# Filling the result with beta's rows: seven transfers moved from GpSimd's queue to SyncE's

## The chip, the cores and the metric

The kernel runs on one core of a Trainium2 chip. The metric is the device time of one execution in microseconds (us). Three executions of the kernel before took 592.14, 590.57 and 588.76 us: the median is 590.57.

## The reference

Two layers of cross attention follow each other. Each takes x (8 batches, 100 rows, 1024 wide) and the same context (8 batches, 1444 rows, 512 wide).

```python
# layer 0
Q = x @ Wq + bq;  K = ctx @ Wk + bk;  V = ctx @ Wv + bv
weights = softmax(Q @ K.T / 32, axis=-1)          # over the context's rows
x = x + (weights @ V) @ Wo + bo
# layer 1
q = x @ Wq + bq;  k = ctx @ Wk + bk;  v = ctx @ Wv + bv
w = softmax(q @ k.T / 32, axis=1)                 # over the 100 query rows
x = w @ v + x
out = (x - mean(x)) * rsqrt(var(x) + 1e-6) * gamma + beta
```

The last line is the one that matters here: beta is added to each row of the result.

## The kernel before, in words

All data is float32. The weights are multiplied together first (Wq with Wk, Wv with Wo), so that the context itself can serve as keys and values. TensorE then goes through layer 0 batch by batch, makes the output product of layer 0 (names o_x, o_y and so on) and the queries of layer 1 (g_x, g_y and so on), goes through layer 1 batch by batch, and ends with output products and the normalisation.

**A batch.** In one pass TensorE makes the scores of a batch against the keys (tile s, line 960, from cT, the context with its features down the partitions) and the rows weighted by the softmax (tile A, line 913, from c, the context with its rows down the partitions). `alternated` (line 1317) lets the two take turns: matmuls of A for batch b stand between matmuls of s for batch b + 2. The first two batches' scores of each layer therefore stand by themselves, ahead of it.

**Loads.** A context block is 1444 by 512, close to 3 MB, and is read anew in each layer in both layouts. `load_features` makes the transfers of cT, `load_rows` those of c; both go through `loaded_in_order` (line 860), which issues them on SyncE's queue and keeps them in program order, so every c and cT load stands at line 861 in the profile. In layer 1 a cT tile comes in four transfers. The tiles live in a pool of ten (`stream`) and one of three (`feature_block`), and SyncE waits before a transfer until TensorE has read what lay there. The built program gives each of SyncE's transfers one of eight DMA semaphores in turn, and each transfer waits for the one that had the semaphore before it, so at most eight of them are on the way.

**The fill.** The result of each batch but the last is stored by GpSimd with an accumulating transfer (line 1247), which adds the normalised rows to what lies in the result. What lies there is beta, written once for seven batches by the transfers of lines 1377 to 1379: each has 100 rows of 1024 (400 KB), all read from the one row of beta in memory, from memory to memory. The last batch is stored by SyncE and ScalarE in two halves (line 1303) and gets its beta from VectorE.

**Order around the change.** On GpSimd's queue stand, in this order: the sums of the softmax weights of layer 0's last batch (lines 1172 to 1177), the seven fills, a memset for the first w of layer 1 (line 972), the load of layer 1's Wv (tile wv, line 1381), two memsets, and from line 185 on the sums of Wv's blocks. On SyncE's queue stand: cT of layer 1's batch 0, cT of batch 1, and then, from `alternated`, by turns c of batch 0 and cT of batch 2, and so on. Two of batch 1's cT tiles are waiting for a buffer that layer 0's output product uses, until 359 us. GpSimd's and SyncE's transfers run on the same 16 DMA engines.

Of the kernel before, what the change touches and what calls it, by code (L numbers as in the profile page):

```python
# [33 lines left out]
B, T, E = 8, 100, 1024  # L34
# [21 lines left out]
def two_layer_cross_attention(ctx: ExitStack, tc: tile.TileContext, a: dict, out: bass.AP):  # L56
    nc = tc.nc
# [10 lines left out]
    def bank(name):  # L68
        return psum.tile([P, 512], F32, tag="ps", name=name)
# [4 lines left out]
    def unit(name):  # L74
        return stream.tile([P, E + L], F32, tag="unit", name=name)
# [7 lines left out]
    def weight_rows(name):  # L83
        return work.tile([P, MC * T], F32, tag="wT", name=name, bufs=3)

    def feature_block(name):
        return work.tile([P, S], F32, tag="prob", name=name, bufs=3)
# [55 lines left out]
    def run(*parts):  # L143

        parts = list(parts)
        while parts:
            parts = [g for g in parts if next(g, parts) is not parts]
# [679 lines left out]
    for g in range(B // G):  # L827
# [3 lines left out]
                out=xT[:, :, g * GT : (g + 1) * GT],  # L831
                in_=a["xT"].rearrange("(c p) t -> p c t", p=P)[:, :, g * GT : (g + 1) * GT],
# [27 lines left out]
    def loaded_in_order(to, src):  # L860
        tc.keep_in_program_order(nc.sync.dma_start(out=to, in_=src))  # L861

    def load_features(b, blocks=(2, 3), parts=2):

        bounds = [LAST * i // parts for i in range(parts)] + [S]

        for k in range(LC):
            name = f"cT_{b}_{k}"
            t = feature_block(name) if k in blocks else unit(name)[:, :S]
            for part in (slice(i, j) for i, j in zip(bounds, bounds[1:])):  # L870
                loaded_in_order(t[:, part], a["ctxT"][b][k * P : (k + 1) * P, part])
            yield t
# [16 lines left out]
    def keys(m):  # L889

        return P if m < MC - 1 else S - LAST
# [3 lines left out]
    def both_sides():  # L895

        return side, 1 - side

    def one_side():

        nonlocal side
        side = 1 - side
        return (1 - side,)
# [40 lines left out]
    def scores_by_keys(s, layer, cT, softmax):  # L944

        b = s["b"]
        q = gT[layer][b // G]
        t0 = b % G * T
        banks = [bank(f"s{layer}_{b}_{n}") for n in range(MC // GM)]
        rest = []  # L950
        for k in range(LC):
            for m in KEYS:
                whole = keys(m) == P
                n = HP if whole else keys(m)
                for h in both_sides() if whole else one_side():
                    o = m * P + h * HP if whole else m * P
                    to = banks[m // GM][h * HP : h * HP + n, m % GM * T : (m % GM + 1) * T]
                    if k >= LC - 2 and not whole:
                        rest.append(to)
                    nc.tensor.matmul(  # L960
                        to,
                        cT[k][:, o : o + n],
                        q[:, k, t0 : t0 + T],
                        start=(k == 0 and m % GM == 0),
                        stop=(k == LC - 1 or (k == LC - 2 and not whole)),
                        skip_group_check=True,
                    )
                if (k, m) != (LC - 1, KEYS[-1]):
                    yield
        w = weight_rows(f"w{layer}_{b}")  # L970
        s["w"] = w[:, : MC * T].rearrange("p (c t) -> p c t", t=T)
        nc.gpsimd.memset(s["w"][:PAD, MC - 1, :], 0.0)  # L972
        s["softmax"] = softmax(s, [blocks_of(banks, ms) for ms in ROWS], rest)
        for _ in islice(s["softmax"], LATER.get((layer, b))):
            pass
        yield

    def blocks_of(banks, ms):

        m, n, r = ms[0], len(ms), keys(ms[0])  # L980
        ps = banks[m // GM][:r, m % GM * T : (m % GM + n) * T]
        return ms, r, ps.rearrange("p (c t) -> p c t", t=T)
# [391 lines left out]
            next(more, None)  # L1374
    run(more)
    vector.in_order = False
    for b in range(B - 1):
        rows = a["L1_xattn_beta"].partition_broadcast(T)
        tc.keep_in_program_order(nc.gpsimd.dma_start(out=out[b], in_=rows))
    wv1 = weights.tile([P, LC, E], F32, tag="w", name="wv1")  # L1380
    nc.gpsimd.dma_start(out=wv1, in_=a["L1_xattn_Wv"].rearrange("(c p) e -> p c e", p=P))


    cT = [list(load_features(0, parts=4)), list(load_features(1, (2,), 4))]
    scores1 = scores_by_keys(batches[0], 1, cT[0], softmax1)
    run(islice(scores1, LC * MC - 2))
    key_bias_rows(kb1, bqbk1)
# [59 lines left out]
```

## Time and profile before

| what | value |
|---|---|
| median of three executions | 590.57 us |
| the profiled execution | 589.33 us |
| its span, first to last instruction | 587.6 us |
| TensorE busy (matmul) | 575.2 us, 98% |
| VectorE, ScalarE, GpSimd busy | 399.6, 133.3, 135.0 us |
| moved by DMA | 142.96 MB, 243 GB/s in the mean |
| the seven fills | issued from 317.5 to 321.4 us, 400 KB each, 9.4 us from issue to landing in the median |
| load of wv | issued at 357.2 us, 10.1 us to landing |
| the last c and cT loads before SyncE's long wait | under way from 359 to about 380 us |

How to read it: the page gives each engine's busy time, then the span cut in 40 slices (14.7 us each) with a digit for the busy tenths. A row of the chain of waits is a start, a length and who held up the end of the program at that moment; "issue" there is time in which an engine waited for nothing that the profile shows. A row of DMA queues is the number of packets, the megabytes, and the time that these packets took as a share of 16 engines over the window. q1 is SyncE's queue, q0 GpSimd's, q10 ScalarE's; q8 and q14 bring instructions. A row of busy time by window gives, for PE, PEld (weight loads), DVE (VectorE), ACT (ScalarE) and POOL (GpSimd), the busy us and the number of instructions, and then TensorE's clock, the DMA engines' busy share and GB/s.

### The profile page before, as it was taken

The numbers are of one execution on the slowest core, as the hardware profiler recorded it, in microseconds if no ns is written. First come the engines' busy times: TensorE is split into PE (matmuls) and PEld (weight loads), VectorE is DVE, ScalarE is ACT, GpSimd is POOL, SyncE is SP. The second block draws the span as 40 slices with busy tenths as digits, with TensorE's granted clock in tenths as the row PEclk, the third lists the DMA queues.
The fourth block names the chain that finished last, engine by engine and source line by source line (L and its number), as shares of the span: only waits on it lengthen the run. The fifth ranks groups of instructions, "written<-read, shape, count | busy, mean of one in ns | idle before, by whom it ended". The sixth has DMA issues, their size and how long they took to land.

```text
span 587.6 us, 17570 instructions
## 1 busy us (share of the span) xinstructions
PE 575.2 (98%) x7470; PEld 497.6 (85%) x7470; DVE 399.6 (68%) x936; ACT 133.3 (23%) x349; POOL 135.0 (23%) x206
## 2 busy tenths in 40 slices
PE   9999999999999999999999899999999999999994
PEld 8887457678899999999998656787999999999992
DVE  1997579879686873876559587876444447664695
ACT  1331321433330112211111000103333303154313
POOL 3110110221111132241225000003922312341052
PEclk9999999999999999999999999999999999999998
DMA  8959989944599999999999605807889997599114
GB/s 274 308 107 321 311 202 296 287 73 97 94 248 360 332 378 365 369 371 366 370 316 289 134 0 206 301 2 222 281 289 304 338 314 258 158 310 328 40 30 85
DMA packets 74313, 142.96 MB, mean 243 GB/s; under 512 B 8572, under 2 KB 30332, under 8 KB 74236
## 3 DMA queue, kind: packets, MB, share of 16 engines
q1 hardware_dynamic: 65790, 117.81, 58.2%
q0 software_dynamic: 8048, 23.57, 19.7%
q8 instruction: 59, 0.97, 0.7%
q10 hardware_dynamic: 398, 0.47, 0.2%
q14 instruction: 18, 0.15, 0.1%
HBM read 124.40 MB, written 6.14 MB: 222 GB/s over the span
## 4 chain that ended last, share of the span: by engine, by line
PE 86%; DMA 6%; SPq 2%; issue 2%; POOL 2%; ACT 1%; DVE 0%; POOLq 0%; DVEq 0%
PE s L960 18%; PE A L913 17%; PE qk_x L166 7%; PE g_x L166 6%; PE o_x L166 5%; PE vo_x L166 4%; DMA cT<-in_ctxT 3%; PE o_y L166 3%; PE g_y L166 3%; DMA c<-in_ctx 3%; PE qk_z L166 2%; PE qk_y L166 2%; SPq L861 2%; PE o_w L166 1%; PE o_z L166 1%
## 5 line engine op out<-in xcount | busy, mean ns | idle before, releaser
L913 PE MATMUL A<-w,c 128*64 128x100 f32 (+1 forms) x3072 | 228.7, 249 | 1.7 <-issue 1.7
L913 PEld LDWEIGHTS A<-w,c 128*64 128x64 f32 (+1 forms) x3072 | 199.1, 137 | 3.6 <-issue 3.3
L960 PE MATMUL s<-g0T,cT 128*64 128x100 f32 (+1 forms) x1472 | 112.7, 249 | 2.0 <-issue 1.9
L960 PE MATMUL s<-g1T,cT 128*64 128x100 f32 (+1 forms) x1472 | 114.1, 249 | 0.1
L960 PEld LDWEIGHTS s<-g1T,cT 128*64 128x64 f32 (+1 forms) x1472 | 97.7, 136 | 2.6 <-issue 1.8
L960 PEld LDWEIGHTS s<-g0T,cT 128*64 128x64 f32 (+1 forms) x1472 | 96.8, 136 | 3.4 <-issue 2.7
L1172 POOL TENSOR_TENSOR part<-w 128x500 f32<-128x500 f32 x16 | 26.4, 1653 | 124.3 <-ACT w L1020 60.9
L1152 ACT ACTIVATE w<-w,negmax 128x100 f32<-128x100 f32 x96 | 35.0, 366 | 68.2 <-DVE negmax L99 68.2
L99 DVE SCALAR_TENSOR_TENSOR w<-s,kb 128x400 f32<-128x400 f32 (+2 forms) x32 | 13.9, 463 | 37.5 <-PE s L960 37.3
L1020 ACT ACTIVATE w<-w 128x400 f32<-128x400 f32 (+2 forms) x32 | 12.0, 442 | 120.3 <-DVE w L99 107.2
L99 DVE TENSOR_REDUCE most<-s 128x100 f32<-128x400 f32 (+1 forms) x24 | 12.5, 520 | 36.5 <-PE s L960 36.5
L166 PE MATMUL qk_x<-qk 128*128 128x256 f32 x128 | 31.0, 392 | 0.0
L166 PEld LDWEIGHTS qk_x<-qk 128*128 128x128 f32 x128 | 24.3, 198 | 3.3 <-ACT qk L440 0.2
L972 POOL MEMSET w<- 68x100 f32 x16 | 3.8, 237 | 75.3 <-PE A L913 36.4
L1232 DVE SCALAR_TENSOR_TENSOR z<-vectors,r,z 100x512 f32<-100x512 f32 x16 | 11.4, 743 | 11.8 <-PE z L1230 11.7
L99 DVE TENSOR_TENSOR w<-w,rtotal 128x400 f32<-128x400 f32 (+2 forms) x32 | 18.3, 570 | 1.1
L1245 ACT ACTIVATE z<-z,rstd 100x1024 f32<-100x1024 f32 x7 | 8.1, 1150 | 45.0 <-POOL rstd L1243 45.0
L1152 ACT ACTIVATION_READ_ACCUMULATOR w<-w,negmax 128x1 f32 x96 | 18.1, 188 | 0.0
L99 DVE TENSOR_TENSOR xT<-xT,o_x 128x400 f32<-128x400 f32 (+1 forms) x32 | 15.9, 538 | 2.8 <-PE o_x L166 2.4
L674 ACT ACTIVATE g1T<-g_x,k 128x400 f32<-128x400 f32 x4 | 2.4, 594 | 61.4 <-PE g_x L166 61.2
L578 POOL DMA_DIRECT2D qk_L_xattn_bk<-qk_L_xattn_bk x6 | 5.2, 922 | 47.8 <-DMA qk_L_xattn_bk<-qk_L_xattn_bk 18.9
L166 PE MATMUL vo_x<-vo 128*128 128x512 f32 x32 | 15.3, 595 | 0.0
(435 smaller groups left out, 1052.7 us busy)
## 6 DMA issues: line engine op xcount, KB each, us to landing
c<-in_ctx SPq DMA_DIRECT2D x176, 256.0 KB
cT<-in_ctxT SPq DMA_DIRECT2D x96, 176.0 KB
cT<-in_ctxT SPq DMA_DIRECT2D x32, 370.0 KB
cT<-in_ctxT SPq DMA_DIRECT2D x32, 352.0 KB
cT<-in_ctxT SPq DMA_DIRECT2D x32, 194.0 KB
vo<-in_L_xattn_Wo SPq DMA_DIRECT2D x8, 512.0 KB
qk<-in_L_xattn_WqT SPq DMA_DIRECT2D x8, 512.0 KB
qk<-in_L_xattn_WqT SPq DMA_DIRECT2D x15, 256.0 KB
```

The lines of the kernel that those rows point to most:

```text
L99: ins = getattr(nc.vector, op)(*args, **kw)
L166: nc.tensor.matmul(banks[n // per][:, n % per * width : (n % per + 1) * width], lhs[i][:, n * P : (n + 1) * P], rhs[i], start=(fresh and i ...
L578: nc.gpsimd.dma_start(out=to, in_=t, accum_op=ALU.add)
L861: tc.keep_in_program_order(nc.sync.dma_start(out=to, in_=src))
L913: nc.tensor.matmul(ps[h * HP : (h + 1) * HP, k * T : (k + 1) * T], c[m // CQ][:r, m % CQ, k * P + h * HP : k * P + (h + 1) * HP], w[:r, m, :],
L960: nc.tensor.matmul(to, cT[k][:, o : o + n], q[:, k, t0 : t0 + T], start=(k == 0 and m % GM == 0), stop=(k == LC - 1 or (k == LC - 2 and no ...
L972: nc.gpsimd.memset(s["w"][:PAD, MC - 1, :], 0.0)
L1020: nc.scalar.activation(rows, rows, AF.Exp)
L1152: nc.scalar.activation(rows[:, i, :], rows[:, i, :], AF.Exp, bias=negmax[:, i : i + 1], accum_out=total[:, i : i + 1])
L1172: add(part, w[:, 0:5, :], w[:, 5:10, :], ALU.add)
L1232: nc.vector.scalar_tensor_tensor(z[:, half], bv1[j][:T], s["r"], ps[:T, :], ALU.mult, ALU.add)
L1245: nc.scalar.activation(z, z, AF.Copy, scale=rstd)
```

## The change

The seven fills leave GpSimd's queue. They are issued by SyncE, in the same way as the context's loads, behind the cT transfers of layer 1's first two batches and ahead of the first c transfer of layer 1. Source, destination, size and number of the transfers stay as they are. The built program has them at that place on SyncE's queue, each with one of the eight semaphores in turn, so that the transfers behind them get other semaphores than before.

```diff
-    for b in range(B - 1):
-        rows = a["L1_xattn_beta"].partition_broadcast(T)
-        tc.keep_in_program_order(nc.gpsimd.dma_start(out=out[b], in_=rows))
     wv1 = weights.tile([P, LC, E], F32, tag="w", name="wv1")
     nc.gpsimd.dma_start(out=wv1, in_=a["L1_xattn_Wv"].rearrange("(c p) e -> p c e", p=P))


     cT = [list(load_features(0, parts=4)), list(load_features(1, (2,), 4))]
+    for b in range(B - 1):
+        loaded_in_order(out[b], a["L1_xattn_beta"].partition_broadcast(T))
     scores1 = scores_by_keys(batches[0], 1, cT[0], softmax1)
```

## The prediction

> **What bounds the kernel now.** The page first: its engine line and the DMA rows by slice.
>
> ```profile
> span 587.6 us, 17570 instructions
> PE 575.2 (98%) x7470; PEld 497.6 (85%) x7470; DVE 399.6 (68%) x936; ACT 133.3 (23%) x349; POOL 135.0 (23%) x206
> ...
> PE   9999999999999999999999899999999999999994
> ...
> DMA  8959989944599999999999605807889997599114
> ```
>
> TensorE is busy 575.2 of 587.6 us, so the whole span holds 12.4 us in which it stands still. One slice before the last shows an 8 (slice 22 counted from 0, 14.7 us each: 323 to 338 us), and in the same slice the DMA row falls from 9 to 6. So I asked the chain of waits, in order of time, for that stretch, and then the timeline of GpSimd.
>
> ```profile
> 319.39 7.70 PE A L913 x175
> 327.09 1.65 issue
> 328.74 1.03 PE A L913 x17
> ```
>
> ```profile
> 317.46 3.85 POOL L1379 DMA_DIRECT2D out<-in_L_xattn_beta  x7
> 329.89 0.18 POOL L972 MEMSET w<- 68x100 f32 x1 [8.58 <-issue]
> ```
>
> The first shows the only stop of TensorE between 221 us and the end that is worth naming: 1.65 us in the last weighted rows of layer 0, "issue", that is with nothing in the profile that it waited for (the list of waits gives TensorE 1.65 us here and 1.9 us in three stops of layer 0, and nothing else past the start). The second shows the seven fills, 3.85 us of issuing on GpSimd. They run while the stop happens. I then asked for the DMA queues in three windows: all of the fills (317 to 335), from 311 to 326, and from 326 to the stop.
>
> ```profile
> q0 software_dynamic: 896, 2.87, 69.8%
> q1 hardware_dynamic: 568, 0.72, 11.1%
> q8 instruction: 2, 0.03, 0.8%
> ```
>
> ```profile
> q1 hardware_dynamic: 2006, 2.57, 52.5%
> q0 software_dynamic: 459, 1.52, 43.2%
> ```
>
> ```profile
> q0 software_dynamic: 72, 0.23, 98.1%
> q8 instruction: 1, 0.02, 7.0%
> ```
>
> q8 brings instructions, 16 KB at a time (0.97 MB in 59 packets on the page; TensorE's 14,940 records over 59 are 253 a block). From 311 to 326 no block comes at all, though TensorE has been eating them since 319.4. One comes at 326 to 327, between fill packets that take 98% of the engines, and TensorE stands from 327.09 until it can be used. Arithmetic: 175 matmuls and as many weight loads in 7.70 us are 45 a us, a block of 256 lasts 5.6 us, two last 11.3 us. From 311 to 327.09 TensorE had used about 64 records of the output products and 350 of these, so it had lived from what was fetched before 311, and then had nothing.
>
> **What the Trainium skill says.** Runtime: NRT & Kernel Launch, section Instruction fetch mechanics: instructions come in 16 KiB blocks of 256 over a DMA queue, fetched ahead while the current ones run; the trace agrees (0.02 MB packets, a stop after two blocks' worth). DMA: Bandwidth & Descriptors, section Queues, rings and completion order: each DMA engine goes round the queues that have work, a whole packet at a time; the trace agrees in so far as the block came late only among fill packets. Same page, Issuing engines are not separate DMA queues: who issues only saves issue time, the engines are the same; so the fills' bytes don't vanish, they move. Same page, Why a DMA increments its semaphore by 16 and not by 1: a transfer from SyncE of 100 rows uses 10 engines, one from GpSimd may use nearly all. The end of the trace agrees: the two 100-row stores there, from SyncE and ScalarE, leave 20 small completion packets, ten each.
>
> ```profile
> DMA packets 221, 0.42 MB, mean 91 GB/s; under 512 B 20, under 2 KB 20, under 8 KB 220
> ```
>
> **The change part by part.**
>
> Removed: seven DMA issues on GpSimd, 3.85 us. Behind them there stand the memset for w and wv1's load. The memset runs at 329.89, just after TensorE's last product of the old w (chain: 328.74 + 1.03); wv1 runs at 357.2 after 27.2 us of waiting for TensorE's o_x. Neither was held by the fills: worth nothing, covered by those waits.
>
> Removed: 2.87 MB of fill packets from 317.5 to about 333. In this stretch SyncE's loads end at 321 and the next wait for buffers until 359, so the DMA engines then stand empty. The instruction block due near 322 (128 records of slow products and A, then 128 more at 45 a us, after the block that the window 309 to 310.5 shows) comes at once. The stop goes: -1.65 us. What is late next there? Nothing that the chain shows; the products behind it (329.9 to 390.8) run back to back. Bounds: 0 if the stop has another cause, -1.65 if all of it goes.
>
> Added: seven issues in SyncE's queue behind cT of the second batch, that is at 366.5 in place of the first c loads of layer 1, some 0.43 us each, 3 us. Queued behind them on SyncE: c and cT of the next batches. Each issue on SyncE also waits for the transfer eight before it (the built program has eight DMA semaphores in turn), so those loads queue behind the fills. Two views tell what that may cost: busy time by window, and SyncE's waits from 359 to 397 us and from 396 to 426.5 us.
>
> ```profile
> 359.00:380.00 21.00, 21.00 (x78) 13.81 (x77) 15.56 (x30) 2.37 (x4) 0.17 (x1) 1.00 0.99 353
> 380.00:397.00 17.00, 17.00 (x192) 14.09 (x193) 13.28 (x23) 2.90 (x6) 0.18 (x1) 1.00 0.01 2
> ```
>
> ```profile
> SPq L861 <- PE s L960: 20.5, 1, 20.5
> ```
>
> ```profile
> SPq L861 <- PE s L960: 28.6, 5, 20.5
> ```
>
> The loads behind the second batch's blocks are done at 379.5; then the DMA is empty for 17 us (share 0.01), because SyncE waits until 396.96 for TensorE to free a block. It waits 28.6 - 20.5 = 8.1 us more, in four pieces, before 426. So the cover is 17.5 + 8.1 = 25.6 us. The first of the loads held up, c of batch 0, is read at 413.9.
>
> How long do the fills take there? Engine time from the row above: 69.8% of 16 engines over 18 us are 201 engine-us, 0.287 us a row of 4 KB. On ten engines that is 20.1 us. The lower bound is ten engines at the rate of the loads of 360 to 380 (362 GB/s by 16): 226 GB/s, 12.7 us. I take 20; both ends lie under 25.6. The loads that ended at 379.5 end at 392 to 400, SyncE's next wait shrinks, and from 426 on nothing differs: cost 0. That cover is not to be wasted: from 426.35 to 475.5 the chain runs over the DMAs and SyncE's queue to a matmul at 475.55, so there a late transfer is paid in full.
>
> Moved: the fills now lie beside instruction blocks of 359 to 390. TensorE takes (78 + 77) records in 21 us there, 7 a us: a block lasts 35 us, and a block late by 5 us costs nothing. From 390.7 on scores run at 45 a us; if fills or held-up loads still fill the DMA then, up to 0.7 us can be lost (the stops of layer 0's scores beside loads were 0.7 at most). From 430 to 470 TensorE lived well with full DMA; I take 0. The later accumulating stores onto the filled rows start at 507, over 100 us after the fills.
>
> Sum: -1.65 us against the profiled execution's 589.33 (span 587.6 and 1.7 around it): 587.7. The three runs have a median of 590.57, 1.24 above it. I set the four executions together, mean 590.2, less 1.65: **588.5 us**.
>
> **The rivals.**
>
> A, as above: 588.5. Chance 0.52; own range 586.8 to 590.2 (half of the 3.4 us over which the runs lie).
>
> B, the stop isn't the fills' doing, or it comes back beside the scores at 390: 590.2. For it: three stops of 0.5 to 0.7 us in layer 0's scores happen with no fills at all. Against: from 430 to 470 eight blocks come (q8 row of that window) with DMA full of loads, and TensorE never stops. Chance 0.14.
>
> C, the stop is longer without the profiler: the runs differ by 3.4 us, the profiled one is near their fast end, and if the difference is this stop, then the median run has 1.65 + 1.24 = 2.9 us of it and all fall to 587.7 or below, with the slowest losing 4.5: 585.7 to 587.7, taken at 587. Chance 0.21. For it: a stop that hangs on where a block lands among 700 rows of fills varies. Against: runs vary by such amounts for other reasons.
>
> D, slower: the fills on ten engines hold back the loads of layer 1. Ten engines read the same beta row, and may need half as long again as on GpSimd's queue, 30.2 us; less the cover of 25.6 that is 4.6 us late at 426, carried by the DMA chain to 475.5: 590.2 - 1.65 + 4.6 = 593.1. It decides from 25.6 us of fills on, and from 27.3 us it beats the gain. Against it: 20.1 us is already the pessimistic reading of the page. Chance 0.13.
>
> That the change doesn't do what it says can be left out: the built program shows the seven transfers on SyncE after cT of batch 1 and gone from GpSimd.
>
> **How the numbers follow.** The bound of 0.5% is 2.95 us, about what a measurement of this kernel can tell from no change: below 587.6 is faster, above 593.5 slower. Faster: of C some 0.16, of A's lower end 0.12: 0.28. Slower: most of D, 0.09. The same: 0.63. Range: 585.8 to 592.2 leaves out D's upper part and the ends of C, some 0.15.
>
> **What would show it.** Right: no "issue" stop near 327; an instruction block near 322; fills of 13 to 20 us that start near 365; the DMA row full until 392 to 400 and SyncE's wait of 20.5 us cut by as much; the first A of layer 1 at 412, 1.65 us earlier. Wrong: the stop stays at 327 without fills (B); TensorE waits for c or cT between 414 and 480, or SyncE no longer waits for TensorE before 426 (D).

## The result, and the profile after

The changed kernel takes 587.86 us (median of 15 runs, 585.15 to 589.50), the kernel before 590.57 us (median of 15 runs beside it, 588.19 to 596.78). The ratio is 0.9953, with a 95% interval of 0.9935 to 0.9971: 2.8 us less, give or take 1.1. Each experiment below has its own runs of the kernel before beside it (medians 590.28, 591.12 and 591.59 us), and a ratio is taken only from runs within 1.5% of the fastest of their kernel, so it is not the quotient of two printed medians. The prediction was 588.5 us in a range of 585.8 to 592.2, with no change beyond 0.5% as the likeliest class.

The page of the changed kernel, the same rows as before:

```profile
span 584.2 us, 17566 instructions
PE 573.8 (98%) x7470; PEld 497.0 (85%) x7470; DVE 399.8 (68%) x936; ACT 133.3 (23%) x349; POOL 131.4 (22%) x199
...
PE   9999999999999999999999999999999999999994
...
DMA  8959989944499999999998006767889997699114
```

The 8 in TensorE's row is gone, and the DMA row, which showed 6 0 in slices 22 and 23, now shows 0 0: the fills have left that stretch. GpSimd has seven instructions less. The chain of waits of the changed kernel from 308 to 334 us:

```profile
310.40 2.88 PE o_x L166 x8
...
318.74 8.39 PE A L913 x192
...
327.31 2.88 PE o_x L166 x8
```

The last A of layer 0 now runs through, 192 matmuls in 8.39 us. Before, the same 192 took 7.70 + 1.65 + 1.03 = 10.38 us. So the stop cost 1.99 us, a little more than the 1.65 us shown as "issue", because the 17 matmuls behind it were slow too. The DMA queues of the changed kernel from 311 to 326 us:

```profile
q1 hardware_dynamic: 2070, 2.66, 52.4%
q8 instruction: 1, 0.02, 0.5%
```

Before, this window held no instruction block (q8); now there is one, and a narrower window puts its start between 320 and 321 us.

The pair of profiles differs by 3.4 us. The starts in the chain tell where. The first o_x starts at 310.40 in place of 311.05: 0.65 us that lie ahead of anything the change touches. The o_x behind A starts at 327.31 in place of 329.95: another 1.99 us, the stop. The last rows of the middle stretch (wsum_ps) come at 476.43 in place of 479.73: 0.66 us more, from the stretch in which before's chain ran over the DMAs. In the other two profiles of the kernel before (below) that last piece is missing, so I count it as chance.

In the new place, SyncE's own waits from 350 to 397 us in the changed kernel (name of the waiting engine and line, of the one waited for, then us in total, times, longest):

```profile
SPq L861 <- PE o_q_x L166: 39.5, 1, 39.5
SPq L861 <- DMA out<-in_L_xattn_beta: 8.0, 5, 2.4
SPq L861 <- PE s L960: 7.2, 1, 7.2
```

The wait for TensorE's scores, 20.5 us before, has become 7.2. SyncE waits 8.0 us for the fills instead, as its eight semaphores come round. TensorE waits for nothing from 310 to 480 us.

### The profile page after: what moved, and what is told of

Read it like the earlier page. It is cut to its first block, busy times and chain, and to the rows that moved or that the text cites. A ratio compares the mean times of both kernels' runs of the same rounds, so it can differ in the third digit from the quotient of the medians.

```text
span 584.2 us, 17566 instructions
## 1 busy us (share of the span) xinstructions
PE 573.8 (98%) x7470; PEld 497.0 (85%) x7470; DVE 399.8 (68%) x936; ACT 133.3 (23%) x349; POOL 131.4 (22%) x199
## 4 chain that ended last, share of the span: by engine, by line
PE 95%; POOL 2%; issue 1%; ACT 1%; DVE 0%; POOLq 0%; DVEq 0%
PE s L960 22%; PE A L913 21%; PE qk_x L166 7%; PE g_x L166 6%; PE o_x L166 5%; PE vo_x L166 4%; PE o_y L166 3%; PE g_y L166 3%; PE qk_z L166 2%; PE qk_y L166 2%; PE o_w L166 1%; PE o_z L166 1%; PE qk_w L166 1%; PE vo_z L166 1%; PE vo_y L166 1%
## 5 line engine op out<-in xcount | busy, mean ns | idle before, releaser
L913 PE MATMUL A<-w,c 128*64 128x100 f32 (+1 forms) x3072 | 228.0, 249 | 0.0
L913 PEld LDWEIGHTS A<-w,c 128*64 128x64 f32 (+1 forms) x3072 | 201.8, 137 | 2.0 <-issue 1.6
L960 PEld LDWEIGHTS s<-g0T,cT 128*64 128x64 f32 (+1 forms) x1472 | 99.9, 136 | 3.0 <-issue 2.4
```

What stands on the lines that cost most here:

```text
L913: nc.tensor.matmul(ps[h * HP : (h + 1) * HP, k * T : (k + 1) * T], c[m // CQ][:r, m % CQ, k * P + h * HP : k * P + (h + 1) * HP], w[:r, m, :],
L960: nc.tensor.matmul(to, cT[k][:, o : o + n], q[:, k, t0 : t0 + T], start=(k == 0 and m % GM == 0), stop=(k == LC - 1 or (k == LC - 2 and no ...
```

## Experiments

Theory F is the prediction's: the fills' packets delay an instruction block that TensorE needs, and the new place is covered. The rivals: the stop has another cause (N), GpSimd's queue costs at any time (Q), the stop varies (C), and the new place costs (D).

**Without the fills.** The kernel before with lines 1377 to 1379 left out, so beta's rows are missing in the result.

```diff
-    for b in range(B - 1):
-        rows = a["L1_xattn_beta"].partition_broadcast(T)
-        tc.keep_in_program_order(nc.gpsimd.dma_start(out=out[b], in_=rows))
```

> Leaves the seven fills out altogether (beta's rows are then missing under the accumulating stores). Theory F (the fills' packets on GpSimd's queue delay the instruction block that TensorE needs near 322 us, and the new place costs nothing): no stop near 327, and the time of the changed kernel, 0.995 of before, within 0.001. If the new place costs something too: faster than the changed kernel, 0.991 or below. Theory N (the gain has nothing to do with a stop at 327): any time, with the stop at 327 still there.

Measured: 586.95 us, ratio to before 0.9954 (0.9936 to 0.9972), the same as the changed kernel. No stop: its chain has "319.42 8.39 PE A L913 x192". So what the fills cost in their old place is all that can be had, and the new place costs nothing that these runs can tell. (Both ratios carry about 1.1 us either way, so a cost of up to some 1.5 us would not show.) D falls for seven fills.

**The fills on GpSimd, but later.** Behind wv1's load, so that they are issued from 356.6 to 360 us.

```diff
+    wv1 = weights.tile([P, LC, E], F32, tag="w", name="wv1")
+    tc.keep_in_program_order(
+        nc.gpsimd.dma_start(out=wv1, in_=a["L1_xattn_Wv"].rearrange("(c p) e -> p c e", p=P))
+    )
     for b in range(B - 1):
         rows = a["L1_xattn_beta"].partition_broadcast(T)
         tc.keep_in_program_order(nc.gpsimd.dma_start(out=out[b], in_=rows))
-    wv1 = weights.tile([P, LC, E], F32, tag="w", name="wv1")
-    nc.gpsimd.dma_start(out=wv1, in_=a["L1_xattn_Wv"].rearrange("(c p) e -> p c e", p=P))
```

> The fills stay on GpSimd's queue, but behind wv1's load, so that they start at 358 us. Theory F: it is the time and not the queue; TensorE takes 7 instructions a us there, no stop of 1 us or more, 0.995 of before. Theory Q (GpSimd's queue itself is what costs, at any time): the gain is lost, 0.999 to 1.001, with a stop between 358 and 400 us.

Measured: 587.55 us, 0.9966 (0.9947 to 0.9985), A in 8.39 us, no stop between 310 and 400. The same queue with the same bytes, 40 us later, does no harm that shows: TensorE takes (70 + 69) instructions in the 18 us from 357 on, some 8 a us, against 45 in A. Q falls.

**ScalarE at the old time.**

```diff
+    for b in range(B - 1):
+        rows = a["L1_xattn_beta"].partition_broadcast(T)
+        tc.keep_in_program_order(nc.scalar.dma_start(out=out[b], in_=rows))
     next(o0)
     next(queries1)
     run(o0)
```

with the three lines on GpSimd taken out.

> The fills at the old time, but issued by ScalarE (from 312 us on, behind its last exponential of layer 0). Theory F in its wide form (fill packets of any queue delay the block): a stop near 327 of 0.5 to 2 us stays, 0.998 to 1.000 of before. In its narrow form (only the packets of GpSimd's queue do): no stop, 0.995.

Measured: 588.38 us, 0.9969 (0.9947 to 0.9990), A in 8.39 us. No stop, as the narrow form has it. But ScalarE issued its fills one by one from 312.9 to 329.5 us, some 2.8 us apart, too thin a stream to settle it.

**SyncE at the old time.** Seven at once, ahead of the cT tiles that wait for a buffer, with the three lines on GpSimd taken out.

```diff
-    cT = [list(load_features(0, parts=4)), list(load_features(1, (2,), 4))]
+    cT = [list(load_features(0, parts=4))]
+    second = load_features(1, (2,), 4)
+    cT.append([next(second), next(second)])
+    for b in range(B - 1):
+        loaded_in_order(out[b], a["L1_xattn_beta"].partition_broadcast(T))
+    cT[1] += second
```

> SyncE issues the seven fills at the old time, ahead of the two cT tiles that wait for a buffer until 359 us, so that up to seven are on the way at once from about 316 us on. Theory F in its wide form (fill packets of any dense queue delay the instruction block; ScalarE's had been too thin): the stop near 327 comes back, 1.5 us or more, 0.998 to 1.000 of before. In its narrow form (only packets on GpSimd's queue delay it): no stop, 0.995 to 0.997.

Measured: 587.42 us, 0.9941 (0.9921 to 0.9962). The DMA queues from 321 to 333 us, this kernel first and then the kernel before:

```profile
q1 hardware_dynamic: 691, 2.56, 58.9%
q8 instruction: 2, 0.03, 1.1%
```

```profile
q0 software_dynamic: 744, 2.35, 89.9%
q8 instruction: 1, 0.02, 0.6%
```

As many fill bytes in the same twelve microseconds, and two instruction blocks come instead of one. Its chain has the whole A in one piece again:

```profile
319.50 8.39 PE A L913 x192
```

So of the two forms the narrow one has the stop right. But "no stop" is not "no delay": SyncE's fills held the block up too, by less than TensorE could bear (the table behind the next experiment). Why GpSimd's hold it up longer is open: on SyncE's queue the fills hold ten engines of 16 (58.9% is close to 10/16), on GpSimd's nearly all (89.9%), and these runs don't separate the queue from the engines it fills.

**Three at the old time, four at the new.**

```diff
-    for b in range(B - 1):
+    for b in range(3):
         rows = a["L1_xattn_beta"].partition_broadcast(T)
         tc.keep_in_program_order(nc.gpsimd.dma_start(out=out[b], in_=rows))
...
+    for b in range(3, B - 1):
+        loaded_in_order(out[b], a["L1_xattn_beta"].partition_broadcast(T))
```

> Three fills stay on GpSimd at the old time, four are issued by SyncE at the new place. Theory F: three fills are through by about 325 us; the block comes some 2 us late in place of 4, which its slack of about 3 us covers: no stop, 0.995 to 0.996. If the cost goes with the number of fills: a stop of 0.7 us, 0.998.

Measured: 588.52 us, 0.9978 (0.9954 to 1.0002): unclear by the time. The profile is clearer: "319.34 8.39 PE A L913 x192", no stop at all. A backlog of three is covered by what TensorE has fetched ahead, seven are not. The cost is not in proportion to the fills.

**Where the block lands in all these kernels.** The traces have every block's packet on q8. Counted from the first matmul of the last A of layer 0, the next block starts and lands at these times:

| fills on the way beside this A | block starts, us | block has landed, us |
|---|---|---|
| none (seven profiles) | 1.9 to 2.1 | 2.9 to 3.3 |
| from ScalarE, one by one | 3.0 | 4.0 |
| from SyncE, seven at once | 3.6 | 4.8 |
| from GpSimd, three | 5.1 | 6.1 |
| from GpSimd, seven (three profiles) | 6.9 to 7.8 | 8.1 to 9.3 |
| from GpSimd, fourteen | 7.7 | 8.9 |

TensorE is through with its 175 matmuls after 7.7 us. In the last two rows the block lands later than that, TensorE stops, and it goes on 1.0 to 1.3 us after the landing; in all other rows the block lands sooner, and there is no stop. So fills from every queue delay the block, GpSimd's the most (about 5 to 6 us for seven, against 1.5 to 2 for SyncE's), and the wide form of F has the delay right. An estimate from the chain says when the block is asked for: 350 records of this A run before the stop, and less a block of 256 that leaves 94, at 45 a us the first 2.1 us. That is where the block starts when no fills are beside it, so it is as if the fetch began when TensorE enters the block before it.

**The kernel before, profiled twice more, and the changed one once more.** No edit.

> The kernel before, unchanged, profiled once more. If the stop hangs on where the block lands among the fills by chance (rival C): a stop near 327 anywhere from 0 to 4 us. If its length is set by the order of the queues: 1.4 to 2.0 us again, at the same matmul.

> The kernel before, unchanged, profiled a third time. Theory F: the stop after the 175th matmul of the last A, 1.6 to 2.2 us; the second loss, that of the first o_x behind it, in some profiles and not in others (0 or about 1.7 us).

> The changed kernel, unchanged, profiled once more. Theory F: no stop between 310 and 400 us. The stops of layer 0 between 190 and 245 us are free to differ by 1 to 2 us from the first profile; if they do, they and not the change are what spreads the runs.

One execution each: 588.28, 591.34 and 585.89 us. The chain of waits from 308 to 334 us of the second profile of before:

```profile
317.00 7.70 PE A L913 x175
324.69 2.13 issue
326.82 1.03 PE A L913 x17
...
328.03 4.58 PE o_x L166 x8
```

and of the third, from 315 to 345 us:

```profile
318.55 7.70 PE A L913 x175
326.25 2.49 issue
328.74 1.03 PE A L913 x17
...
329.96 4.51 PE o_x L166 x8
```

The stop comes after the 175th matmul in every profile that has seven fills on GpSimd at the old time, at whatever time it comes, so it hangs on an instruction and not on a moment. Counted over TensorE's matmuls and weight loads it is behind the 7762nd record each time. The "issue" stops of layer 0 of 0.3 us and more in these three profiles come behind records 2174, 2683, 2938, 3192 and 4716. From one of these to the next, and from the last to 7762, it is 2, 1, 1, 6 and 12 times 254 records, to within two; the prediction had counted 253 records a block. So all these stops lie at the edge of an instruction block, those of layer 0, which rival B named, as well.

The length of the stop varies, 1.65, 2.13, 2.49 us. And in two of three profiles there is a second loss that is not shown as waiting at all: the eight products o_x behind A take 4.58 and 4.51 us where they take 2.88 in every other profile, 1.6 to 1.7 us more. The windows show what it is. First the second profile of before, then the first one:

```profile
328.20:331.60 3.40, 3.40 (x6) 1.74 (x6) 3.25 (x6) 0.00 (x0) 0.00 (x0) 0.50 0.62 135
```

```profile
330.00:333.00 3.00, 3.00 (x9) 1.70 (x10) 2.93 (x6) 0.00 (x0) 0.07 (x1) 1.00 0.64 150
```

TensorE's granted clock (the third number from the end) is 0.50 for 3.4 us, in the third profile too, from 329.8 on; at half the clock, 3.4 us cost 1.7. In the other twelve profiles the clock is 1.00 here. Both stretches begin 1.1 to 1.4 us after TensorE goes on, so they look like a consequence of the stop. But after a stop of 2.21 us (next experiment) none follows, and these runs don't show what decides. All in all the three profiles lose 1.99, 4.2 and 4.5 us (all rows of A and o_x against 8.39 and 2.88), a mean of 3.5. The changed kernel's second profile shows A in 8.39 and o_x in 2.88 us.

**The fills twice at the old place.** `for b in [*range(B - 1), *range(B - 1)]:` at line 1377; the second set writes the same rows again.

> GpSimd issues the seven fills twice over at the old place (the second set writes the same rows again), so that fill packets last from 317 to about 347 us. Theory F: the stop near 327 as before, 1.6 to 2.2 us, and now each later block that TensorE needs before 347 us comes late too: one or two more losses of about 1.7 us, like the one at 331 us in the second profile of the kernel before: 1.000 to 1.005 of before. If the cost went with the bytes: 1.004 to 1.005. If it is one fixed stop: 1.000.

Measured: 591.01 us, 1.000 (0.9983 to 1.0017), with this chain:

```profile
319.66 7.70 PE A L913 x175
327.36 2.21 issue
329.57 1.03 PE A L913 x17
...
330.78 2.88 PE o_x L166 x8
```

The same stop, no more. The block behind it comes late too, at 339.8 us, 10 us after TensorE went on, but these products take few instructions, and TensorE never waits for it. The other 2.87 MB, issued up to 335 us, cost nothing: the loss doesn't go with the bytes.

**The fills twice and three times at the new place.** The loop over `range(B - 1)` in the changed kernel runs over it two or three times.

> SyncE issues the seven fills twice over at the new place (the second set writes the same rows again), so that 14.7 us of fills on ten engines become about 29. By the prediction's cover of 25.6 us: SyncE no longer waits for TensorE before 426, loads come 3 to 4 us late, TensorE waits for them between 440 and 480: 1.005 of the changed kernel, 1.000 to 1.002 of before. If the cover is larger: 0.995 to 0.997 of before. If the fills cost in proportion at this place: slower than before by more than 0.3%.

> SyncE issues the seven fills three times over at the new place, some 44 us of fills. By the kernel with two sets, whose fills lasted 30 us and used up all of SyncE's waits for TensorE before 426 without a stop of TensorE: 14 us more must show as TensorE waiting for c or cT between 400 and 480 us, 10 to 16 us in all, 1.015 to 1.025 of before. If fills at this place are hidden without limit: 0.996 to 1.000.

Twice: 589.16 us, 0.9987 (0.9962 to 1.0012), between what was expected of the two covers; its runs spread from 586.4 to 594.6, and its profile (586.76 us) has no wait of TensorE for a load. SyncE waits for TensorE's scores for 0.2 us in all from 396 to 426.5: the cover is used up almost to the last. Three times (four runs): 602.41 us, 1.0201 (1.0169 to 1.0233), and TensorE waits:

```profile
PE s L960 <- DMA cT<-in_ctxT: 9.5, 5, 3.2
```

The DMA queues of this kernel from 376 to 396 us, where nearly nothing but fills is on the way:

```profile
DMA packets 1112, 4.15 MB, mean 207 GB/s; under 512 B 102, under 2 KB 102, under 8 KB 1111
...
q1 hardware_dynamic: 1111, 4.13, 63.8%
```

4.13 MB are 1008 rows; 63.8% of 16 engines for 20 us are 204 engine-us, 0.202 us a row. Ten engines of 16 are 62.5%: the ten are busy without a break. By that rate seven fills take 700 times 0.202 by 10, 14.2 us. From the first 4 KB packet to the last, the traces have 14.9 us for one set, 30.3 for two and 43.8 for three. The ratios 1.0201 and 0.9953 put three sets 14.6 us behind one set. Taken as it is, that leaves a cover of about 29 us. But only 9.5 of the 14.6 us are waits for cT. Another 3.4 are lost in two stretches of 3.4 us at a granted clock of 0.50 (from 416.8 and from 474.8 us), which follow the two longest waits, and the rest I can't place. By the waits alone the cover is about 34 us. Two sets lie near its lower end: the profiled execution has no wait, and three of the four slowest have mean clocks of 0.990 and 0.993, so these probably did stop.

**ScalarE in the empty stretch.** With the three lines on GpSimd taken out:

```diff
+    after_A = const.tile([P, 1], F32, tag="after_A", name="after_A")
+    tc.keep_in_program_order(nc.scalar.copy(after_A, A0[1][:, 0, GT - 1 : GT]))
+    for b in range(B - 1):
+        rows = a["L1_xattn_beta"].partition_broadcast(T)
+        tc.keep_in_program_order(nc.scalar.dma_start(out=out[b], in_=rows))
     next(o0)
```

> ScalarE issues the fills at 331 us: a one-column copy ahead of them waits for the last A of layer 0. They then lie in the stretch from 331 to 357 us in which the DMA engines are empty, and SyncE's loads don't queue behind them. Theory F: no stop, 0.994 to 0.995 of before, the same as the changed kernel, since its loads were covered anyway. If the changed kernel pays for its place: faster than it, 0.991 to 0.993.

Measured: 587.10 us, 0.9965 (0.9943 to 0.9987). SyncE has its 20.4 us of waiting back, and it is worth nothing. No version here beats the changed kernel beyond the intervals.

## Why the prediction was right

- **The stop at 327 us goes, with the fills as its cause: right.** Seven or more fills on GpSimd there: a stop, in four profiles of four. None, three, or seven from another queue or at another time: none, in ten profiles of ten. That it is the instruction block that comes late is read from the q8 packets: the block lands behind the 7.7 us of A in those four profiles and ahead of them in the ten, and the stop lies at the edge of a block. No run changed the block alone. (Two readings of the prediction are loose: "two blocks' worth", where its own count of 414 records is 1.6 blocks, and a block late "only among fill packets", since layer 0's stops beside loads lie at block edges too.)
- **The size, -1.65 us: too small.** The term was one stop of one profiled execution. Measured are 2.8 us (1.7 to 3.8). The stop varies from 1.65 to 2.49 us, the slow rows behind it add 0.3, and in two of three profiles half the clock for 3.4 us adds 1.6 to 1.7. The sentence "the products behind it run back to back" was true of the profile shown and not of the other two. That 588.5 lies so near 587.86 is in part luck: the prediction started from 590.2, 0.4 us below the median of 590.57, which made up for some of the missing 1.1.
- **Rival C had the size best (2.9 us for the median run), but not the reason.** It isn't the profiler: two profiled executions lose 4.2 and 4.5 us. And C took the stop for the whole spread of the runs, which is wrong: the first o_x, ahead of which nothing differs between the kernels, starts anywhere from 308.65 to 312.48 us in the 14 profiles. That is about as much as the runs of the changed kernel spread (585.15 to 589.50). The kernel before spreads more (588.19 to 596.78 us), as the varying stop and the half clock would have it.
- **The seven issues on SyncE cost nothing: right.** Without any fills the time is the same. The issues took 0.75 us each where the prediction had 0.43, and the fills 14.9 us where it took 20 (bounds 12.7 and 20.1): I had carried over GpSimd's 0.287 us a row, and SyncE's rows take 0.202. Both are under the cover. The wait of 20.5 us shrank by 13.3. DMA is near empty again (share 0.04) from 390 us, a little ahead of 392 to 400.
- **The cover of 25.6 us and the price beyond it (D): the mechanism right, the cover too small.** It is 29 to 34 us. What goes beyond it is paid, and two stretches at half the clock come on top.
- **"The fills' bytes don't vanish, they move": right; but I thought all queues alike for a waiting instruction block.** The same fills at the same time from SyncE hold it up 1.5 to 2 us, from GpSimd 5 to 6.
- **First A of layer 1 at 412: it starts at 411.2.** Of the 0.8 us between, 0.65 is the earlier start of this execution.

## What to carry to other kernels

A stop of TensorE under "issue", in a stretch of many short matmuls, is worth a look at the DMA rows that bring instructions: count what TensorE eats, see if a block is missing from the window, and compare when the block lands with when it is needed. No stop doesn't mean no delay. A background transfer is better put where the engine eats few instructions, and its new place is priced by the waits of the queue it is put into, up to the point where those waits are used up. One profile gives the place of a stop but not its mean size: profile the kernel before two or three times before its length goes into a sum, and read the granted clock behind the stop.

## What the runs showed that I had not expected

- Fills from memory to memory take 0.202 us a 4 KB row on SyncE's queue (ten engines) and 0.287 us on GpSimd's (nearly all 16). From first packet to last, seven take 14.9 us in the changed kernel and 14.7 in the kernel before: six engines more bring nothing here.
- Some lost time shows in no wait: eight products in 4.58 us in place of 2.88, with TensorE counted as busy throughout. It shows in the granted clock, 0.50 for 3.4 us behind a stop of 2.13 or 2.49 us.
- 14 fills on GpSimd at the old place cost no more than seven.
